# Other slots for the side work of two state-space scans: softplus additions, MLP halves, the parts of B, output additions, and one SiLU

## The chip, the cores and the metric

The kernel is one program on one core of a Trainium2 chip. Its inputs and outputs lie in the chip's memory. The metric is the device time of a whole execution in microseconds (us), the median of several runs; lower is better.

## The reference, cut to what matters

Four images of 256 channels and 64 x 64 points pass through four layers, each with a residual addition. Layers 0 and 1 are attention layers, which the change does not touch. Layers 2 and 3 are state-space ("Mamba") layers; layer 3 treats the 256 channels as four groups of 64 that share their weights, and an MLP follows its scan. What the scan computes in both, for every channel d and each of 16 states n:

```python
delta = softplus(dt @ dt_proj_w + dt_proj_b)      # dt, B, C: projections of u
h     = exp(delta * A[n]) * h + (delta * u) * B[n]   # over the 4096 points
y    += C[n] * h                                     # summed over n
y     = (y + u * D) * silu(z)                        # then out_proj
```

In the grouped layer there follow, per group, a normalisation, `gelu(m @ fc1 + b) @ fc2`, and at the end a 256 x 256 convolution with SiLU and the residual addition.

## The kernel before, in words

The four images are computed one after the other: two attention layers, the first state-space layer (`mamba_layer`), the grouped one (`grouped_mamba_layer`). All data are float32 on 128 partitions (channels); a stretch of 1024 points is a chunk, half of it (512) is what one matmul writes.

**Slots.** `scan_blocks` runs both scans. A block is 128 channels of one chunk; a slot is one state n of one block, so a layer has 16 blocks x 16 slots = 256 slots for an image. In a slot, VectorE multiplies delta*u into B's row (`pb`, L915) and runs the recurrence (`h`, L921); GpSimd multiplies by C (`hc`, L927); TensorE adds `hc`, transposed, into PSUM (`turn`, L873, tile `y`); ScalarE makes the decay of a slot three ahead (`da`, L857) and keeps the last column of the slot before (`m_state`, L862). TensorE spreads B's row over the partitions (`spread`, L845) two slots ahead. In three of a block's 16 slots, those in `apart` (0, 4 and 8 in the grouped layer), the row of B comes by DMA instead (tile `bb`) and GpSimd multiplies it (L831), issued two slots ahead; the decay of these slots goes to PSUM (`dap`).

**Order.** The schedule is manual: every engine's order is the order of the program text. A slot issues, in this order: `pb`, `h`, the GpSimd product for slot i+2, `hc`, the decay for slot i+3, `m_state`, the DMA loads of C and B, the background steps of the slot, `spread` for i+2, `turn` for i-1, and `dap` for i+2. In slot 1 of a block (`ends[0]`) the copies of the previous block's y out of PSUM (L884) stand behind the background steps; y has one buffer, so the new block's first `turn` waits for them.

**Background steps.** `blk["bg"]` is a dictionary from slot to steps; `put(block, slots, steps)` fills it by hand. The steps that matter here:

- `x_proj` (through `table_steps`): projections to B, C and dt (tile `m_bct`), then B split in bf16 parts: ScalarE copies (`m_parts`, L1082) and GpSimd subtractions (L1085), in turn: copy, subtraction, copy, subtraction.
- `delta` (`delta_steps`): for each half of the chunk a matmul (`dt_ps`), three ScalarE functions (L1044 to L1046) and VectorE's addition (L1050), which also ends the use of the PSUM buffer; then delta*u on GpSimd (L1054).
- `mlp`: out projection and its square (L1654, L1655), the deviation (L955, L956), a scale on GpSimd (L1664), first MLP half (`hidden(0)`, `gelu(0)`), second half (`hidden(1)`, `gelu(1)`), then `fc2` in two steps. `hidden` needs both buffers of the PSUM tag `mm`, so the second half's matmuls wait for the first half's GELU.
- `out_conv`, `out_silu`, `out`: the closing convolution, its SiLU, the addition of x on GpSimd (L1743) and the store, which SyncE issues in its own order.
- `silu`: SiLU of z or u, between two loads of ScalarE's function tables.

In the grouped layer two blocks, an "even" and an "odd" one, form a pair (chunk k, column c); an image has 8 pairs, numbered 0 to 7, of 32 slots. The even block's slots carry `x_proj` and `delta` of the odd block, the MLP of the pair before, and for c = 1 the output of the chunk before and the normalisation of the chunk to come; the odd block's slots carry u, `x_proj` and `delta` for the next pair's even block.

Of the kernel before, what the change touches and what calls it, by code (L numbers as in the profile page):

```python
# [8 lines left out]
F32 = mybir.dt.float32  # L9
# [9 lines left out]
P = 128  # L19
# [8 lines left out]
NT = 512  # L28
# [16 lines left out]
class Net:  # L45
# [757 lines left out]
    def scan_blocks(self, blocks, loop, psum, psb, psy, apart, ends, first, last=None):  # L803
# [109 lines left out]
        for i, (blk, n) in enumerate(slots):  # L913
            if not is_apart(i):
                nc.vector.tensor_tensor(pb[i], blk["du"], pb[i], ALU.mult)  # L915
            h[i] = loop.tile([P, NC], F32, tag="h", name="h", bufs=3)
            for ss in pieces(i):
                state = 0.0 if blk["first"] else blk["state"](n)
                if ss.start:
                    state = h[i][:, ss.start - 1 : ss.start]  # L920
                nc.vector.tensor_tensor_scan(  # L921
                    h[i][:, ss], da[i][:, ss], pb[i][:, ss], state, ALU.mult, ALU.add
                )
            product(i + 2)
            hc[i] = loop.tile([P, NC], F32, tag="hc", name="hc", bufs=3)
            for ss in pieces(i):
                nc.gpsimd.tensor_tensor(hc[i][:, ss], h[i][:, ss], cb[i][:, ss], ALU.mult)  # L927
            decay(i + 3)
            keep(i - 1)
            load_c(i + 3)  # L930
            load_b(i + 4)
            if i >= DS and n != ends[0]:
                end(slots[i - DS][0], n)
            for step in blk["bg"].get(n, ()):
                step()
            if i >= DS and n == ends[0]:
                end(slots[i - DS][0], n)
            spread(i + 2)
            turn(i - 1)
            decay(i + 2, True)  # L940
            for d in (pb, da, cb):
                del d[i]
# [173 lines left out]
    def mamba_layer(self, x, bridge, pe_dram, w_in, w_cw, w_x, w_dt, w_out, v_dram):  # L1116
        tc, nc = self.tc, self.nc
        ND = 4
        with ExitStack() as ctx:
# [122 lines left out]
            def silu(*what):  # L1242
                def step():
                    for k, d, key in what:
                        t = chunks[k]["blocks"][d][key]
                        nc.scalar.activation(t, t, AF.Silu)
                    self.exp_ln_tables()

                return step
# [102 lines left out]
            for k in range(n_chunk):  # L1352
# [3 lines left out]
                def put(d, where, steps):  # L1356
                    for i, f in zip(where, steps):
                        bg[d].setdefault(i, []).append(f)
# [5 lines left out]
                        put(0, where, out_proj(k - 1, i // 2, i % 2))  # L1364
                put(0, (9, 10, 11, 12, 12), delta(k, 1))
                put(0, (14, 15), (in_z(k, 0, 0), in_z(k, 0, 1)))
                put(1, (1,), (silu((k, 0, "zs")),))
                put(1, (6, 7, 8, 9, 10), delta(k, 2))
                put(1, (11, 12), (in_z(k, 1, 0), in_z(k, 1, 1)))
                put(1, (14,), (silu((k, 1, "zs")),))  # L1370
# [127 lines left out]
    def grouped_mamba_layer(self, x, bridge, begun, ws_dram, outc_dram, v_dram, out_b, load):  # L1498
        tc, nc = self.tc, self.nc
        w_in, w_cw, w_x, w_dt, w_out, w_f1, w_f2 = ws_dram  # L1500
        with ExitStack() as ctx:
# [140 lines left out]
            def mlp(k, c, s):  # L1642
                ss = slice(s * NT, s * NT + NT)
                box = {}
# [33 lines left out]
                            box["hid"][:, f, g], box["ps"][g], AF.Gelu, bias=f1b[:, f : f + 1]  # L1678
                        )

                def fc1():
                    box["hid"] = work.tile([P, 2, 2, NT], F32, tag="hid", name="hid", bufs=1)
                    gelu(0)
                    hidden(1)
                    gelu(1)
                    self.exp_ln_tables()

                def fc2(f):
                    if f == 0:
# [16 lines left out]
                        )  # L1706

                return (
                    out_proj, deviation, scale, lambda: hidden(0), fc1,
                    lambda: fc2(0), lambda: fc2(1),  # L1710
                )


# [145 lines left out]
            for i, (k, c) in enumerate(pairs):  # L1859
# [12 lines left out]
                if more:  # L1872
# [2 lines left out]
                    put(even, (0, 1, 4, 5, 6), h0)  # L1875
                    put(even, (14, 15), h1)
                    put(odd, (1, 2, 3), h1[2:])
                put(even, (4, 5, 6, 7, 8, 9), x_proj(k, 2 * c + 1))
                if i:
                    m0, m1 = mlp(*pairs[i - 1], 0), mlp(*pairs[i - 1], 1)  # L1880
                    put(even, (5, 6, 7, 10, 11, 12, 13), m0)
                    put(even, (6, 7, 8), m1)
                    if c == 0:
                        put(even, (14, 15), m1[3:])
                        put(odd, (0, 1), m1[5:])
                    elif i + 1 < len(pairs):
                        put(odd, (15,), m1[3:])
                        late.append(((0, 1, 1), m1[4:]))
                    else:
                        put(odd, (3, 4, 5, 6), m1[3:])  # L1890
                put(even, (7, 8, 8, 9, 10), delta(k, 2 * c + 1))
                also = [lambda k=k: out_silu(k - 1)] if c == 1 and k else []
                if i == 0:
                    put(even, (1, 2), [in_z(0, 0, s) for s in range(2)])
# [2 lines left out]
                    also = [lambda blk=odd: silu_of(blk, "u")]  # L1897
                put(even, (3,), (silu(k, c, "zs", also),))
                if c == 1 and k:
                    put(even, (4, 4, 5, 5), [out(k - 1, *sm) for sm in outs])  # L1900
                    put(even, (8,), [lambda k=k: load(slice((k - 1) * NC, k * NC))])
                if c == 0 and k:
                    put(odd, (10, 12, 15), [out_conv(k - 1, *sm) for sm in outs[:3]])
                    late.append(((0,), [out_conv(k - 1, *outs[3])]))

                if i + 1 < len(pairs):
                    nk, ncol = pairs[i + 1]
                    put(odd, (4, 5, 6, 7), all_u(nk, ncol))
                    put(odd, (7,), (silu(nk, ncol, "u"),))
                    put(odd, (8, 8, 8, 9, 10, 11), x_proj(nk, 2 * ncol))  # L1910
                    put(odd, (9, 10, 10, 11, 12), delta(nk, 2 * ncol))
                    put(odd, (13, 14), [in_z(nk, ncol, s) for s in range(2)])
            self.scan_blocks(
                [blk for c in chunks for blk in c["blocks"]], loop, psum, psb, psy, (0, 4, 8),
# [164 lines left out]
```

## Time and profile before

| | |
|---|---|
| median of 3 runs | 12054.86 us (12047.85 to 12070.48) |
| the profiled execution's own time | 12068.31 us |
| its span in the profile | 12066.5 us |
| VectorE (DVE) busy | 9840.1 us, 82% |
| TensorE (PE) busy | 9882.3 us, 82% |
| GpSimd (POOL) busy | 8887.9 us, 74% |
| ScalarE (ACT) busy | 7053.7 us, 58% |
| scan of the first state-space layer, first image | 1028.4 to 1968.5, 940.1 us |
| scan of the grouped layer, first image | 2023.0 to 2991.4, 968.4 us |

Busy times are shares of the whole span; the four images repeat the same pattern. "Idle before <-X" names what ended an engine's idle time. PE's busy time is that of pipelined matmuls and says little about how near its limit it is. In the lines of a timeline the columns are the start (us from the span's start), the duration, the engine, the line of the code, the operation, what it writes and reads, how many were merged, and the idle time before it with its releaser.

### The profile page before, as it was taken

What the parts mean: (1) busy time and instruction counts of PE and PEld (TensorE: products, weight loads), DVE (VectorE), ACT (ScalarE), POOL (GpSimd) and SP (SyncE); (2) the same over time, 40 slices, a digit from 0 to 9 for tenths busy, and PEclk for the clock granted to TensorE, in tenths of its full rate; (3) what the DMA queues carried; (4) which work ended last, traced back from release to release, by engine and by line L of the source; (5) the groups of instructions that cost most, each with busy time, mean ns of one, the idle gap of its engine ahead of it and who ended that gap; (6) DMA issues with size and microseconds to landing.
All of it is one profiled execution on the core that took longest, in us unless ns stands there. A gap on an engine that the chain in (4) does not pass through costs nothing. (4 is left out here: it accounts for less than half of the span.)

```text
span 12066.5 us, 192470 instructions
## 1 busy us (share of the span) xinstructions
PE 9882.3 (82%) x70624; PEld 5634.8 (47%) x71104; DVE 9840.1 (82%) x8322; ACT 7053.7 (58%) x13064; POOL 8887.9 (74%) x6082
## 2 busy tenths in 40 slices
PE   8887887777888888777789878877778987887777
PEld 4554554444455455444445545544434554554443
DVE  6667998988666799898866679989886677998898
ACT  4555554776455555477645555547764565555776
POOL 3666886888366688688836668868883666886887
PEclk9998998999999899899899989989999998998899
DMA  3343554454334455445433445544543344554444
GB/s 92 103 126 136 172 175 145 168 175 159 86 102 125 136 173 174 146 169 177 156 86 105 123 135 173 174 147 168 175 159 86 103 127 135 173 176 145 169 171 152
DMA packets 682832, 1742.12 MB, mean 144 GB/s; under 512 B 89217, under 2 KB 195217, under 8 KB 681633
## 3 DMA queue, kind: packets, MB, share of 16 engines
q1 hardware_dynamic: 676768, 1721.39, 43.9%
q8 instruction: 563, 9.22, 0.3%
q10 hardware_dynamic: 5120, 8.39, 0.3%
q14 instruction: 381, 3.11, 0.1%
HBM read 1601.51 MB, written 94.37 MB: 141 GB/s over the span
## 5 line engine op out<-in xcount | busy, mean ns | idle before, releaser
L927 POOL TENSOR_TENSOR hc<-h,cb 128x1024 f32<-128x1024 f32 x2056 | 4813.0, 2350 | 908.1 <-DVE h L921 383.3
L921 DVE TENSOR_TENSOR_SCAN h<-da,m_state,pb 128x1024 f32<-128x1024 f32 x1248 | 2920.2, 2340 | 161.9 <-DVE pb L915 2.9
L873 PE MATMUL y<-ident,hc 128*128 128x128 f32 x16384 | 2340.8, 291 | 373.2 <-POOL hc L927 246.9
L873 PEld LDWEIGHTS y<-ident,hc 128*128 128x128 f32 x16384 | 2065.1, 151 | 983.2 <-POOL hc L927 402.4
L915 DVE TENSOR_TENSOR pb<-du,pb 128x1024 f32<-128x1024 f32 x1672 | 2024.8, 1211 | 103.2 <-PE pb L845 72.0
L857 ACT ACTIVATE da<-delta,m_v 128x1024 f32<-128x1024 f32 x1672 | 1898.4, 1141 | 163.0 <-DVE h L921 147.1
L845 PE MATMUL pb<-m_parts,pick 128*128 128x512 bf16 x2832 | 965.4, 411 | 817.6 <-DVE h L921 759.3
L519 POOL TENSOR_SCALAR pr<-pr,sm,zero 128x256 f32<-128x256 f32 x2048 | 1126.4, 568 | 429.4 <-DVE sm L516 381.3
L504 ACT ACTIVATE pr<-sc,mn 128x256 f32<-128x256 f32 x2048 | 959.6, 493 | 728.0 <-DVE mn L493 396.2
L845 PEld LDWEIGHTS <-pick 128*128 128x128 bf16 x3312 | 256.6, 100 | 1824.9 <-DVE h L921 1069.9
L921 DVE TENSOR_TENSOR_SCAN h<-da,pb 128x1024 f32<-128x1024 f32 x424 | 969.7, 2287 | 55.8 <-DVE pb L915 1.9
L831 POOL TENSOR_TENSOR bb<-du,bb 128x1024 f32<-128x1024 f32 x376 | 889.3, 2365 | 76.9 <-DMA bb<-m_cd 70.8
L493 DVE TENSOR_REDUCE mn<-sc 128x4 f32<-128x1024 f32 x512 | 609.4, 1219 | 361.8 <-PE sc L483 361.5
L921 DVE TENSOR_TENSOR_SCAN h<-dap,m_state,bb 128x1024 f32<-128x1024 f32 x288 | 671.8, 2333 | 69.8 <-ACT dap L857 59.1
L532 PE MATMUL pt_ps<-ident,pr 128*128 128x128 f32 x4096 | 591.8, 286 | 134.2 <-ACT pts L545 99.3
L204 PE MATMUL conv_ps<-att_y,att_wb 128*128 128x512 f32 x1536 | 692.9, 595 | 5.3 <-DVE gn_mean L151 5.3
L532 PEld LDWEIGHTS pt_ps<-ident,pr 128*128 128x128 f32 x4096 | 461.5, 145 | 361.5 <-POOL tap L225 93.6
L857 ACT ACTIVATE dap<-delta,m_v 128x1024 f32<-128x1024 f32 x376 | 419.7, 1116 | 357.1 <-DVE h L921 283.5
L483 PE MATMUL sc<-kv,q 32*64 32x128 f32 x16384 | 407.4, 300 | 156.6 <-DMA kv<-kv_dram 103.7
L558 PE MATMUL ov_ps<-pts,kv 128*32 128x64 f32 x16384 | 432.6, 233 | 121.5 <-DVE pts L543 72.7
L240 DVE SCALAR_TENSOR_TENSOR lp<-vimg,att_v,lp 128x512 f32<-128x512 f32 x616 | 465.6, 756 | 28.3 <-DVE lp L240 1.0
L204 PE MATMUL conv_ps<-att_xn,att_wa 128*128 128x512 f32 x1024 | 461.0, 603 | 14.2 <-POOL att_xn L180 14.2
(289 smaller groups left out, 17008.8 us busy)
## 6 DMA issues: line engine op xcount, KB each, us to landing
cb<-m_cd SPq DMA_DIRECT2D x2048, 512.0 KB
kv<-kv_dram SPq DMA_DIRECT2D x1984, 128.0 KB
bb<-m_cd SPq DMA_DIRECT2D x376, 512.0 KB
kv_dram<-kst SPq DMA_DIRECT2D x128, 256.0 KB
kv_dram<-vn SPq DMA_DIRECT2D x128, 256.0 KB
q<-q SPq DMA_DIRECT2D x256, 128.0 KB
m_pe<-in_pe_dram SPq DMA_DIRECT2D x32, 512.0 KB
out_dram<-yo SPq DMA_DIRECT2D x64, 256.0 KB
```

The source lines that it names most:

```text
L204: nc.tensor.matmul(ps, w[:, k, w0 + m * P : w0 + (m + 1) * P], src[:, k], start=(k == 0), stop=(k == 1),)
L493: nc.vector.tensor_reduce(mn[h], sc[h].rearrange("p r w m n -> p (w m) r n"), AX.XY, ALU.min)
L504: nc.scalar.activation(t[:, g].rearrange("p j r t -> p r j t"), sc[h][:, :, g // 2, g % 2, :].rearrange("p r (j t) -> p r j t", j=2), AF.E ...
L519: nc.gpsimd.tensor_scalar(t[:, g], t[:, g], s[:, g : g + 1], self.zero, ALU.mult, ALU.add)
L532: nc.tensor.transpose(pt[h][j][:, g, :], t[:, g, j].rearrange("p r t -> p (r t)"), self.ident,)
L831: nc.gpsimd.tensor_tensor(pb[i], slots[i][0]["du"], pb[i], ALU.mult)
L845: nc.tensor.matmul(pb[i][:, ss], self.pick[:, n : n + 1].to_broadcast([P, P]), blk["parts"][:, ss], start=True, stop=True,)
L857: nc.scalar.activation(da[i], blk["delta"], AF.Exp, scale=blk["a"](n))
L873: nc.tensor.matmul(blk["y"][:, ss], t[:, ss], self.ident, is_transpose=True, start=(n == 0 and ss.start % NT == 0), stop=(n == DS - 1 and ...
L915: nc.vector.tensor_tensor(pb[i], blk["du"], pb[i], ALU.mult)
L921: nc.vector.tensor_tensor_scan(h[i][:, ss], da[i][:, ss], pb[i][:, ss], state, ALU.mult, ALU.add)
L927: nc.gpsimd.tensor_tensor(hc[i][:, ss], h[i][:, ss], cb[i][:, ss], ALU.mult)
```

## The change

A background step may now stand at n + 0.5: it is issued between `spread` and `turn` of its slot. The SiLU of z in the first layer moves from slot 1 to 1.5 of a chunk's second block, behind the copies of y. In the grouped layer the step `fc1` is cut in two, of which the second half stands half a slot or a slot later; the parts of B in the even block move from slots 6, 7, 8, 9 to 9, 11, 12, 13; the first softplus addition moves from slot 8 to 9 (even) and 10 to 11 (odd), beside the second; the four output additions, with their stores, go from slots 4, 4, 5, 5 to 4, 5, 6, 7; and one closing convolution goes from slot 10 to 9 of the odd block. The numbers of instructions are the same on every engine; only their order differs.

```diff
@@ scan_blocks
             spread(i + 2)
+            for step in blk["bg"].get(n + 0.5, ()):
+                step()
             turn(i - 1)
@@ mamba_layer
-                put(1, (1,), (silu((k, 0, "zs")),))
+                put(1, (1.5,), (silu((k, 0, "zs")),))
@@ grouped_mamba_layer, mlp
-                def fc1():
-                    box["hid"] = work.tile([P, 2, 2, NT], F32, tag="hid", name="hid", bufs=1)
-                    gelu(0)
-                    hidden(1)
-                    gelu(1)
-                    self.exp_ln_tables()
+                def fc1(f):
+                    if f == 0:
+                        box["hid"] = work.tile([P, 2, 2, NT], F32, tag="hid", name="hid", bufs=1)
+                    else:
+                        hidden(1)
+                    gelu(f)
+                    if f:
+                        self.exp_ln_tables()
...
-                    out_proj, deviation, scale, lambda: hidden(0), fc1,
-                    lambda: fc2(0), lambda: fc2(1),
+                    out_proj, deviation, scale, lambda: hidden(0), lambda: fc1(0),
+                    lambda: fc1(1), lambda: fc2(0), lambda: fc2(1),
@@ grouped_mamba_layer, the slots
-                put(even, (4, 5, 6, 7, 8, 9), x_proj(k, 2 * c + 1))
+                put(even, (4, 5, 9, 11, 12, 13), x_proj(k, 2 * c + 1))
...
-                    put(even, (5, 6, 7, 10, 11, 12, 13), m0)
+                    put(even, (5, 6, 7, 10, 11, 11.5, 12, 13), m0)
                     put(even, (6, 7, 8), m1)
                     if c == 0:
-                        put(even, (14, 15), m1[3:])
-                        put(odd, (0, 1), m1[5:])
+                        put(even, (14, 15, 15.5), m1[3:])
+                        put(odd, (0, 1), m1[6:])
                     elif i + 1 < len(pairs):
                         put(odd, (15,), m1[3:])
-                        late.append(((0, 1, 1), m1[4:]))
+                        late.append(((0, 0.5, 1, 1), m1[4:]))
                     else:
-                        put(odd, (3, 4, 5, 6), m1[3:])
-                put(even, (7, 8, 8, 9, 10), delta(k, 2 * c + 1))
+                        put(odd, (3, 4, 4.5, 5, 6), m1[3:])
+                put(even, (7, 9, 8, 9, 10), delta(k, 2 * c + 1))
...
-                    put(even, (4, 4, 5, 5), [out(k - 1, *sm) for sm in outs])
+                    put(even, (4, 5, 6, 7), [out(k - 1, *sm) for sm in outs])
...
-                    put(odd, (10, 12, 15), [out_conv(k - 1, *sm) for sm in outs[:3]])
+                    put(odd, (9, 12, 15), [out_conv(k - 1, *sm) for sm in outs[:3]])
...
-                    put(odd, (9, 10, 10, 11, 12), delta(nk, 2 * ncol))
+                    put(odd, (9, 11, 10, 11, 12), delta(nk, 2 * ncol))
```

## The prediction

> **What bounds the kernel now.** From the page's busy times (VectorE and TensorE 82%, GpSimd 74%) I went to busy time by stretch, for the two scans of the first image:
>
> ```profile
> core 0: us, PE busy (x) PEld busy (x) DVE busy (x) ACT busy (x) POOL busy (x), PEclk, DMA share, GB/s
> 1028.40:1968.50 940.10, 799.07 (x3462) 464.47 (x3522) 878.30 (x543) 510.41 (x746) 798.44 (x353) 0.94 0.50 173
> 2023.00:2991.40 968.40, 734.92 (x3425) 407.40 (x3485) 873.45 (x531) 663.57 (x959) 853.10 (x387) 0.91 0.51 171
> ```
>
> The grouped scan has no more VectorE work than the first (873 against 878 us), yet takes 28 us longer. VectorE sets the pace (90% busy), but GpSimd is close behind (88%): what VectorE gains can be lost again to GpSimd. So next, who VectorE waits for in the grouped stretch (us, times, longest):
>
> ```profile
> DVE delta L1050 <- ACT delta L1046: 31.6, 19, 2.5
> DVE h L921 <- ACT dap L857: 12.5, 4, 4.2
> DVE pb L915 <- PE pb L845: 11.5, 8, 4.6
> DVE pb L915 <- PE f_ps L1670: 6.6, 4, 2.2
> DVE m_zs L887 <- PE fin_ps L898: 3.3, 5, 1.0
> ```
>
> About 65 us an image, half of it the softplus addition. The same query in the first layer shows 4.0 us of `m_zs` on `fin_ps` for this image. The rest of the reading is from timelines of the second image. ScalarE and VectorE, pair 3 (c = 1), even block, slots 6 to 9:
>
> ```profile
> 5426.54 1.52 ACT L1005 ACTIVATE m_xn<-m_xn,m_v 128x512 f32<-128x512 f32 x2 [0.96 <-POOL m_xn L998]
> 5427.97 1.04 ACT L1082 ACTIVATE m_parts<-m_bct 128x1024 bf16<-128x1024 f32 x1
> ...
> 5431.10 1.12 ACT L857 ACTIVATE dap<-delta,m_v 128x1024 f32<-128x1024 f32 x1
> ...
> 5432.33 2.35 DVE L921 TENSOR_TENSOR_SCAN h<-dap,m_state,bb 128x1024 f32<-128x1024 f32 x1 [4.26 <-ACT dap L857]
> 5436.85 0.69 DVE L1050 SCALAR_TENSOR_TENSOR delta<-dt_ps,delta 128x512 f32<-128x512 f32 x1 [2.17 <-ACT delta L1046]
> ```
>
> ScalarE works almost without a pause and is late; a copy of parts stands in front of `dap`. The odd block of the same pair, slots 10 and 11:
>
> ```profile
> 5503.96 0.63 ACT L1046 ACTIVATE delta<-delta 128x512 f32<-128x512 f32 x1
> 5504.62 0.69 DVE L1050 SCALAR_TENSOR_TENSOR delta<-dt_ps,delta 128x512 f32<-128x512 f32 x1 [2.48 <-ACT delta L1046]
> 5507.84 0.63 ACT L1046 ACTIVATE delta<-delta 128x512 f32<-128x512 f32 x1
> 5508.81 0.67 DVE L1050 SCALAR_TENSOR_TENSOR delta<-dt_ps,delta 128x512 f32<-128x512 f32 x1
> ```
>
> The second logarithm ends at 5508.47, 0.3 us before its addition starts: the second addition has almost no slack.
>
> **What the Trainium skill says.** "PSUM — Partial Sum Buffer", section "Engine vs sequencer instructions": ScalarE, VectorE and GpSimd take instructions strictly first in, first out, and matmuls keep program order. The trace agrees: `dap` at 5431.10 stands behind work that nobody needs yet. "ScalarE: Activation LUTs", "What ACT_TABLE_LOAD costs": about 1283 ns a load; here 1.28 us, and a SiLU with its two loads 3.65 us. "TensorE: Matmul & The Clock Gate", "Part 1: The HAM clock gate": after an idle window of about 3.4 us matmuls run at half rate. The trace agrees: after PE idles 4.33 us at 5579 to 5584, eight transposes take 1.91 us, later 1.04.
>
> **The change part by part.** No instruction is added or removed on any engine, so every part is a wait that goes, stays or comes.
>
> *Even block, c = 1 (pairs 3, 5).* Copy of the first parts from slot 6 to 9: 1.04 us less ahead of `dap`. One addition of x on GpSimd (1.26) less ahead of the normalisation's scale: the 0.96 wait goes. So `dap` ends 1.9 us earlier, and so does the scan that waits 4.26 for it. The second copy (1.06) also leaves the way of the second half's three functions: their end moves from 5440.86 by 1.9 + 1.05 to about 5437.9. VectorE no longer stops for the first addition; it reaches slot 9's end at about 5437.2, does the first addition (0.67), and waits no more than 0.1 for the second. Both are done near 5438.6 instead of 5441.7: 3.0 us won by slot 10. But GpSimd cannot follow. From 5419.7 to 5466.5 it has one idle gap, 0.85 us, and its work there is unchanged: two subtractions (2.15 + 2.12) leave slots 7 and 9 and come back in 11 and 13, ahead of `bb` for the next block. Its last `hc` of the block can come only 0.85 us earlier. Behind it hang `turn`, the normalisation's matmuls (in program order on PE), the square root on ScalarE, y's copies, `fin_ps` and VectorE's `m_zs` in odd slots 3 and 4. I carry on 1.3 us: 0.85, and some 0.45 because `spread` and the square now come early in this chain.
> *Pair 1* has no output additions, so its 1.01 wait stays; `dap` gains 1.04, and the same chain on GpSimd leaves 0.9. *Pair 7* has no normalisation behind it; there `bb` ends 1 us earlier (GpSimd's 1.02 idle gap), its scan was released 2 us after the present one can be: 1.8.
>
> *Even block, c = 0 (pairs 2, 4, 6).* The copy leaves the queue, and all of the first addition's wait (1.33 to 1.75) goes; the second finds its logarithm done. At slot 15 stands the MLP's first half:
>
> ```profile
> 5583.53 2.65 PE L1670 MATMUL f_ps<-m_sq,m_wf 64*128 64x512 f32 x4 [4.33 <-ACT hid L1677]
> 5586.11 0.61 PE L845 MATMUL pb<-m_parts,pick 128*128 128x512 bf16 x1
> ...
> 5587.19 1.23 DVE L915 TENSOR_TENSOR pb<-du,pb 128x1024 f32<-128x1024 f32 x1 [2.18 <-PE f_ps L1670]
> ```
>
> `spread` waits behind the second half's matmuls, VectorE 2.18 us for it and 1.22 for the next. At 15.5 the matmuls stand behind `spread`: the 2.18 goes; `turn` is 2 us later instead, and `spread` of slot 16 comes about when VectorE wants it (I leave 0.3 to 0.7 of wait). Against it GpSimd's `bb` for odd slot 0, now behind a subtraction, ends at the same time as before: 0.4 of wait. Sum 1.4 + 2.2 + 0.6 - 0.4 - 0.6 = 3.2 (pair 6: 3.0). At 11 and 11.5, and where the halves move across blocks, no VectorE wait existed: nothing, hidden by `spread` two slots ahead.
>
> *Pair 0.* The second addition waits 1.2 for its logarithm behind the second copy: 1.1 goes. Its largest wait (4.6 to 5.5 us for `pb`, behind `x_ps` waiting for SiLU of u) is untouched.
>
> *Odd blocks.* Here the copies of parts stay. From 5492.28 (eviction of u) to 5508.47 ScalarE has no idle, so the second logarithm cannot end sooner. VectorE skips the 2.48, arrives 2.5 earlier at slot 11, and waits some 2.2 there: the wait moves from the first to the second addition. Gain 0.3 in pairs 0, 1, 3, 5; in 2, 4, 6 the convolution ahead of `dt_ps` costs 0.2. The move of the convolution also frees the second `dt_ps` matmul from waiting (1.08 in pair 4) for the PSUM buffer of the first, which the later addition would otherwise lengthen.
>
> Grouped layer, one image: 1.1 + 0.9 + 3.2 + 1.3 + 3.2 + 1.3 + 3.0 + 1.8 + 0.6 = 16.4.
>
> *SyncE's queue.* Stores at slots 6 and 7 hold the loads of C behind them until GpSimd's addition is done, at most some 1.6 us; C is loaded three slots (3 x 3.6 us) ahead: nothing. The tile of `yo` has the one buffer that `hid` takes at slot 11: the last store is issued some 7.5 us before, and the kernel's last store landed within 3 us. Nothing; if that cover went, each us late holds ScalarE at the GELU.
>
> *First layer.* ScalarE and VectorE, second chunk, slots 1 to 3:
>
> ```profile
> 4356.32 1.28 ACT L1246 ACT_TABLE_LOAD   x1
> ...
> 4359.99 1.08 ACT L884 ACTIVATE du<-y 128x512 f32<-128x512 f32 x2
> ...
> 4365.32 0.69 DVE L887 TENSOR_TENSOR m_zs<-fin_ps,m_zs 128x512 f32<-128x512 f32 x1 [2.14 <-PE fin_ps L898]
> ```
>
> y's copies can start when `turn` ends (4356.83), 3.1 us earlier; the 2.14 goes. The SiLU ends some 4361.5, before `m_zs` reads it. By chunk (waits on `fin_ps`): 1.4, 2.1, 1.9 and none: 5.3 an image, with VectorE free of other waits behind, so it stays.
>
> **Sum.** (16.4 + 5.3) x 4 = 87 us. Span 12066.5 - 87 = 11979.5; the profiled execution lies 1.8 us above its span and 13.5 above the median, so 12054.86 - 87 = 11968. What a measurement of this kernel can tell is about 0.2%, 24 us.
>
> **Rivals.** *A, as above*: the odd waits move, GpSimd caps the even ones; gain 40 to 135 us, 11920 to 12015. *B, the waits go altogether*: half of the odd waits too (7 x 1.2 x 4 = 34), and c = 1 keeps its 3.0 (8 x 1.7 = 14), gain 87 + 48 = 135, or 181 if the 11.5 us an image of `pb` on `pb` go as well; 11874 to 11920. For it: the chain has slack at other places; against it: ScalarE's unbroken run. *C, the gains are eaten*: later waits (`fin_ps`, `bb`) take all but the first layer's and a few: 12025 to 12055. *D, slower*: GpSimd idles in slots 8 to 10, where its subtractions were, and is 4.2 us later at `bb` and the block's last `hc`. The present slack of `bb` is 0.8 to 3.3 us; by my working GpSimd idles 0 to 2.9 there. With 2.9 or more in all 32 even blocks, some 2 us are lost in each after slack and first gains: +64 - 21 = +43, about 12098. It decides from an idle time of about 1.5 us beyond what VectorE has won. *E, a step does not do what it says*: only the first layer's or only the MLP's cut acts, -20 to -45: in A's or C's edge.
>
> **Chances.** A 0.64, B 0.13, C with E 0.14, D 0.09. Faster by over 24 us: A, B and a part of C, 0.85; same 0.07; slower 0.08. The range takes A, most of B and the upper edge of C up to 12030: 11895 to 12030; A's own is 11920 to 12015.
>
> **What would show it.** Right: no wait of the first addition; waits of about 2 us at the second addition of odd blocks; `dap` waits of about 2 us in pairs 3 and 5; no `pb` wait on `f_ps`; no `m_zs` wait of 2 us in the first layer; GpSimd above 90% in the grouped scan, which lasts about 952 us, the first 932 to 935. Wrong: GpSimd idle at slots 8 to 10 and `h` waiting for `bb` by over 1 us (D); second additions of odd blocks without wait (B); GELU waiting for a store.

## The result, and the profile after

| | before | after |
|---|---|---|
| median | 12054.86 us | 12005.28 us (11987.04 to 12014.62) |
| the profiled execution's own time | 12068.31 us | 11996.08 us |
| its span | 12066.5 us | 11993.8 us |
| scans of the first state-space layer, mean of the four images | 938.7 us | 938.4 us |
| scans of the grouped layer, mean of the four images | 967.9 us | 951.4 us |

The ratio of the times is 0.9954, with a 95% interval of 0.994 to 0.9969: the kernel is 0.46% faster, some 37 to 72 us with 50 between the medians. The two profiled executions lie 72.2 us apart in their times and 72.7 in their spans, because that of before was 13.45 us above its median and that of after 9.2 us below its own (72.23 - 13.45 - 9.20 = 49.58). Of the 72.7 us, 66.1 are in the four scans of the grouped layer, 1.3 in those of the first layer, and 5 elsewhere.

So the grouped layer gained as much as was forecast (16.5 us an image; the forecast was 16.4), and the first layer did not (0.3 an image; the forecast was 5.3). How much such a mean can tell is seen in kernels whose edit leaves a layer alone: the first layer's scan came to 937.2 to 940.0 us in profiles of kernels that don't touch it (`fc1`, `even`, `odd`, `outs`; 938.7 in before), the grouped scan to 965.0 to 967.3 (`silu`, `light`, `light_silu`; 967.9 in before). A difference of under 1.5 us an image in the first layer, or under 3 in the grouped one, is not clear of that by itself.

Busy time by stretch, the two scans of the first image of after (first layer, then grouped):

```profile
core 0: us, PE busy (x) PEld busy (x) DVE busy (x) ACT busy (x) POOL busy (x), PEclk, DMA share, GB/s
1031.30:1967.70 936.40, 806.89 (x3464) 468.49 (x3524) 878.38 (x543) 510.43 (x746) 798.56 (x353) 0.94 0.49 174
2021.10:2968.80 947.70, 727.18 (x3428) 401.39 (x3486) 873.11 (x531) 662.09 (x959) 852.87 (x387) 0.91 0.51 175
```

The work is unchanged on all engines; the grouped stretch is 20.7 us shorter in this image (14.3 to 16.7 in the others), and GpSimd is now busy for 90% of it. What VectorE waits for in the grouped scan of this image (us, times, longest):

```profile
DVE pb L915 <- PE pb L845: 16.6, 11, 5.5
DVE delta L1052 <- ACT delta L1048: 12.2, 11, 2.3
DVE h L921 <- ACT dap L857: 6.7, 3, 2.2
DVE h L921 <- POOL bb L831: 4.3, 7, 2.3
DVE m_zs L887 <- PE fin_ps L898: 4.0, 8, 0.7
DVE pb L915 <- remote: 2.3, 3, 1.9
```

("remote" stands where the profile does not name what ended the wait.) The softplus addition fell from 31.6 to 12.2 us, the decay `dap` from 12.5 to 6.7, and the 6.6 us of `pb` behind `f_ps` are gone. But `pb` behind B's spread row grew from 11.5 to 16.6, and waits for `bb` grew from 1.3 to 4.3. With the small rows the list sums to 68 us before and 48 in after: VectorE's waits make the whole difference of the two scans.

The even block of pair 3 in the second image, slots 7 to 9, from the timelines of ScalarE and VectorE (the same place as before):

```profile
5398.41 1.52 ACT L1007 ACTIVATE m_xn<-m_xn,m_v 128x512 f32<-128x512 f32 x2
...
5402.02 1.12 ACT L857 ACTIVATE dap<-delta,m_v 128x1024 f32<-128x1024 f32 x1
...
5403.24 2.35 DVE L921 TENSOR_TENSOR_SCAN h<-dap,m_state,bb 128x1024 f32<-128x1024 f32 x1 [2.24 <-ACT dap L857]
...
5409.11 0.67 DVE L1052 SCALAR_TENSOR_TENSOR delta<-dt_ps,delta 128x512 f32<-128x512 f32 x1
5410.32 0.69 DVE L1052 SCALAR_TENSOR_TENSOR delta<-dt_ps,delta 128x512 f32<-128x512 f32 x1 [0.54 <-ACT delta L1048]
```

The copy of parts and the 0.96 us wait of the normalisation are gone from the way to `dap`; the scan waits 2.24 us for it instead of 4.26, the first addition not at all. The odd block of that pair:

```profile
5477.50 0.67 DVE L1052 SCALAR_TENSOR_TENSOR delta<-dt_ps,delta 128x512 f32<-128x512 f32 x1
5480.35 0.69 DVE L1052 SCALAR_TENSOR_TENSOR delta<-dt_ps,delta 128x512 f32<-128x512 f32 x1 [2.18 <-ACT delta L1048]
```

As forecast, the wait of 2.48 at the first addition is now one of 2.18 at the second. And the turn from the even to the odd block in pair 4, where `spread` had waited for the MLP's second half (TensorE, then VectorE):

```profile
5552.29 0.59 PE L845 MATMUL pb<-m_parts,pick 128*128 128x512 bf16 x2 [2.36 <-DVE h L921]
5552.91 1.70 PE L1672 MATMUL f_ps<-m_sq,m_wf 64*128 64x512 f32 x4
5554.73 1.09 PE L873 MATMUL y<-ident,hc 128*128 128x128 f32 x8
...
5554.67 1.21 DVE L915 TENSOR_TENSOR pb<-du,pb 128x1024 f32<-128x1024 f32 x1
```

`spread` goes first, and neither `pb` waits. Here the eight transposes that follow take 1.09 us; before they took 1.91. That turns out to matter.

By pair of the grouped layer, the mean over the four images (us; forecast gains with the odd blocks' terms put in):

| pair | 0 | 1 | 2 | 3 | 4 | 5 | 6 | 7 | sum |
|---|---|---|---|---|---|---|---|---|---|
| before | 119.30 | 122.00 | 120.69 | 124.22 | 121.30 | 124.72 | 119.32 | 116.36 | 967.9 |
| after | 119.61 | 122.03 | 117.41 | 122.46 | 117.01 | 122.21 | 117.05 | 113.60 | 951.4 |
| gain | -0.3 | 0.0 | 3.3 | 1.8 | 4.3 | 2.5 | 2.3 | 2.8 | 16.5 |
| forecast | 1.4 | 1.2 | 3.0 | 1.6 | 3.0 | 1.6 | 2.8 | 1.8 | 16.4 |

### The profile page after: what moved, and what is told of

It is laid out like the page before. It is cut to its first block, busy times and chain, and to the rows that moved or that the text cites. A ratio compares the mean times of both kernels' runs of the same rounds, so it can differ in the third digit from the quotient of the medians.

```text
span 11993.8 us, 192457 instructions
## 1 busy us (share of the span) xinstructions
PE 9862.3 (82%) x70632; PEld 5605.7 (47%) x71104; DVE 9842.8 (82%) x8322; ACT 7047.9 (59%) x13064; POOL 8892.2 (74%) x6082
## 5 line engine op out<-in xcount | busy, mean ns | idle before, releaser
L558 PE MATMUL ov_ps<-pts,kv 128*32 128x64 f32 x16384 | 427.8, 231 | 122.1 <-DVE pts L543 74.1
```

## The experiments

"Scan" below is the mean of the four images' scans in the profiled execution (before: first layer 938.7, grouped 967.9; after: 938.4 and 951.4). Ratios are to the kernel before, on the same chip.

### One part at a time

**silu.** The kernel before with the SiLU's move (and the half slots it needs) alone.

```diff
-                put(1, (1,), (silu((k, 0, "zs")),))
+                put(1, (1.5,), (silu((k, 0, "zs")),))
```

> The kernel before with only the SiLU of the first layer at slot 1.5. Theory (TensorE takes it back): the wait of m_zs on fin_ps in slot 4 of the second block of a chunk (1.4, 2.1, 1.9 us an image) is gone, but pb waits for spread (some 0.7 us at slot 14 of that block) and dap waits longer two blocks on; the first layer's scan keeps 937 to 940 us in every image, the total moves by 0 to -8 us. Rival (the gain is real, and something in the grouped layer lost it): the first layer's scan is 5 us shorter in every image, the total -20 us.

Measured: 12060.93 us, ratio 1.0 (0.9991 to 1.0009); first layer 938.0 us an image, 0.7 less than before and within the spread. So the theory held and the rival fell. What VectorE waits for in the first layer's scan of the first image, before and then in this kernel:

```profile
DVE h L921 <- ACT dap L857: 11.5, 7, 2.9
DVE pb L915 <- PE pb L845: 8.2, 7, 2.8
DVE m_zs L887 <- PE fin_ps L898: 4.0, 2, 2.0
```

```profile
DVE h L921 <- ACT dap L857: 13.1, 8, 2.9
DVE pb L915 <- PE pb L845: 11.9, 12, 2.9
```

The row of `m_zs` is gone, all 4.0 us of it. The other two rows grew by 1.6 and 3.7 us, 5.3 in all; the whole lists, with their small rows, sum to 34.9 and 34.5 us. Over the four images it is 33.7 and 32.5. Where: the timeline of after, second chunk of the second image, ten slots behind the place of the former wait (TensorE, then VectorE):

```profile
4366.89 1.88 PE L1235 MATMUL z_ps<-m_xn,m_wz 128*128 128x512 f32 x4
4368.61 1.88 PE L1210 MATMUL u_ps<-m_xn,m_wxi_w 128*128 128x512 f32 x4
4370.33 0.59 PE L845 MATMUL pb<-m_parts,pick 128*128 128x512 bf16 x2
...
4370.96 1.23 DVE L915 TENSOR_TENSOR pb<-du,pb 128x1024 f32<-128x1024 f32 x1 [0.74 <-PE pb L845]
```

TensorE works through the projections of z and u without a pause, `spread` stands behind them, and VectorE, which now comes earlier, waits. In after and in `silu` alike, the wait for `dap` in the second half of the chunk then grows from 1.3 to some 2.2 us in the second chunk and from 2.4 to 2.9 in the third (means of the four images).

**fc1.** The kernel before with the MLP cut alone.

```diff
-                        put(even, (14, 15), m1[3:])
-                        put(odd, (0, 1), m1[5:])
+                        put(even, (14, 15, 15.5), m1[3:])
+                        put(odd, (0, 1), m1[6:])
...
-                        late.append(((0, 1, 1), m1[4:]))
+                        late.append(((0, 0.5, 1, 1), m1[4:]))
```

> The kernel before with only the MLP's first half cut in two. Theory: the wait of pb on f_ps (2.2 us in pairs 2, 4, 6) and most of the next pb wait are gone; nothing else moves; 3 us in each of these pairs, 9 an image, total -36 us. Rival (GpSimd's bb for odd slot 0 or the later turn takes it): the wait becomes one of h on bb or of m_zs on fin_ps, total 0 to -10 us.

Measured: 12068.11 us, ratio 1.0002 (0.9993 to 1.0011); grouped 968.9. The theory fell; the rival's total about held, but not its cause. The wait of 2.18 us on `f_ps` is gone, but the `pb` of odd slot 2 then waits 3.0 us in pairs 2, 4 and 6, for `spread`. In the grouped scan of the first image of this kernel (11.5 us before):

```profile
DVE pb L915 <- PE pb L845: 15.9, 10, 4.4
```

**even.** The even block's parts of B and first softplus addition alone.

```diff
-                put(even, (4, 5, 6, 7, 8, 9), x_proj(k, 2 * c + 1))
+                put(even, (4, 5, 9, 11, 12, 13), x_proj(k, 2 * c + 1))
...
-                put(even, (7, 8, 8, 9, 10), delta(k, 2 * c + 1))
+                put(even, (7, 9, 8, 9, 10), delta(k, 2 * c + 1))
```

> The kernel before with only the even block's parts of B and softplus addition in their new slots. Theory: pairs 2, 4, 6 gain 1.4 us each, pairs 3 and 5 gain 3 us by slot 10 and keep 1.3 of it because GpSimd runs without idle time from slot 4 to the next block; pairs 0, 1, 7 about 1 each; 10 an image, total -40 us. Rival D (GpSimd idles where its subtractions were and is late at bb): the even blocks end no earlier or later, total 0 to +40 us.

Measured: 12041.51 us, ratio 0.9979 (0.9972 to 0.9987); grouped 962.0, a gain of 5.9 where 10 were expected. Pairs 2, 4 and 6 gained 2.3, 2.8 and 1.5, pair 7 1.6; pair 3 gained nothing, pair 5 1.0, and pairs 0 and 1 lost 1.9 and 1.4. In pairs 3 and 5 slot 8 waits 3.3 us for whichever comes last, `dap` or GpSimd's `bb`: 4.24 less only 0.9. Behind it the chain that the prediction follows from GpSimd's last `hc` shows: `m_zs` in odd slot 4 waits 2.0 us for `fin_ps` there, against 0.5 and 0.9 before.

**odd.** The odd block's first softplus addition and the convolution alone.

```diff
-                    put(odd, (10, 12, 15), [out_conv(k - 1, *sm) for sm in outs[:3]])
+                    put(odd, (9, 12, 15), [out_conv(k - 1, *sm) for sm in outs[:3]])
...
-                    put(odd, (9, 10, 10, 11, 12), delta(nk, 2 * ncol))
+                    put(odd, (9, 11, 10, 11, 12), delta(nk, 2 * ncol))
```

> The kernel before with only the odd block's softplus addition at slot 11 and the convolution at slot 9. Theory (ScalarE's run from the SiLU of u to the second logarithm sets the time): the first addition no longer waits, the second waits 1 to 2.3 us in every odd block, the grouped scan is as long as before within 4 us, total 0 +- 12 us. Rival (the waits of 2.4 us are gone): grouped scan 15 us shorter, total -60 us.

Measured: 12049.58 us, ratio 0.9983 (0.9975 to 0.9991); grouped 964.9, a gain of 3.0. The waits moved to the second addition (1.0 to 2.2 us each), as the forecast had it. In pairs 2, 4 and 6 the `pb` ahead of it now waits 1.3 to 1.4 us as well; with these the odd blocks' waits at this place fell by only 1.0 us an image (16.5 to 15.5), so the rest of the 3.0 has its place elsewhere, at waits that also change from profile to profile.

**outs.** The four output additions alone, from slots 4, 4, 5, 5 to 4, 5, 6, 7.

```diff
-                    put(even, (4, 4, 5, 5), [out(k - 1, *sm) for sm in outs])
+                    put(even, (4, 5, 6, 7), [out(k - 1, *sm) for sm in outs])
```

> The kernel before with only the four output additions at slots 4 to 7. Theory (ScalarE's order sets dap, one addition less ahead of the norm's scale saves the wait of 0.96): the dap wait of pairs 3 and 5 falls from 4.2 to about 3.3 us, the bb wait of pair 7 (1.3 us) goes, 2 to 3 us an image, total -8 to -12 us. Rival (GpSimd's order is not what dap waits for): same waits, total 0 +- 4 us. Second rival: the later store holds the GELU of slot 11, total above +10 us.

Measured: 12067.45 us, ratio 1.0 (0.9991 to 1.0008), so no gain in time; grouped 966.3, a gain of 1.6, nearly all of it in pair 7 (1.8). In pairs 3 and 5 slot 8 now waits 3.18 us instead of 4.24, as expected, but for GpSimd's `hc`, and these pairs end no earlier (-0.1 and 0.3): `m_zs` in odd slot 4 waits 1.7 to 1.9 us.

The parts alone gain, in the grouped layer, -1.0, 5.9, 3.0 and 1.6 us an image: 9.5 of the 16.5 that they gain together. These are readings of one profile for each kernel. The times don't settle it: the ratios of the five parts add up to 0.36%, with 0.07 to 0.09% of doubt on each, and the whole is 0.46% (0.31 to 0.60). That the parts act on one another is read from the places, pair by pair, below.

### Two parts together, and TensorE's rate

**even_fc1.** `even` and `fc1` together.

> The kernel before with the even block's moves and the MLP's first half cut in two together. Alone they gave -6.3 us an image and 0. Theory (with the copies gone, ScalarE reaches the GELU of slot 15 earlier, so spread and the second half's matmuls both come in time): the pb waits of odd slots 1 and 2 in pairs 2, 4, 6 (1.5 to 2 us with the even moves alone, 3 us with the cut alone) are gone, grouped scan 5 us shorter than with the even moves alone, total -45 us. Rival (the two only add): grouped scan as with the even moves alone, total -26 us.

Measured: 12040.96 us, ratio 0.9983 (0.9974 to 0.9992); grouped 962.2, as `even` alone. The theory fell, the rival held: still nothing for the MLP cut. In pairs 2, 4 and 6 the second `pb` of the odd block waits 1.8 us. The same turn of blocks in pair 4 as shown of after (TensorE, then VectorE):

```profile
5576.96 0.59 PE L845 MATMUL pb<-m_parts,pick 128*128 128x512 bf16 x2 [3.16 <-DVE h L921]
5577.58 2.09 PE L1672 MATMUL f_ps<-m_sq,m_wf 64*128 64x512 f32 x4
5579.60 1.97 PE L873 MATMUL y<-ident,hc 128*128 128x128 f32 x8
5581.36 1.44 PE L1697 MATMUL f_ps<-m_xn,m_skip 128*128 128x512 f32 x2
...
5584.38 1.23 DVE L915 TENSOR_TENSOR pb<-du,pb 128x1024 f32<-128x1024 f32 x1 [1.36 <-remote]
```

The order of the work is that of after. But TensorE had been idle for 3.16 us instead of 2.36, and the same matmuls then took 2.09, 1.97 and 1.44 us instead of 1.70, 1.09 and 1.02; the next `spread` comes late, and VectorE waits for it.

I read this place in all 12 cases (pairs 2, 4 and 6 of four images) of each kernel, and sorted them by the rate of the eight transposes:

| kernel | at full rate (about 1.09 us) | their waits of `pb` | at half rate (about 1.97 us) | their waits of `pb` |
|---|---|---|---|---|
| fc1 | none | | 12, after 3.6 us idle | 3.04 |
| even_fc1 | none | | 12, after 3.1 to 3.2 us idle | 1.79 |
| after | 8, after 2.3 to 2.5 us idle | 0.00 | 4, after 3.1 to 3.2 us idle | 1.88 |
| even_fc1_warm (below) | 8, after 1.3 to 2.1 us idle | 0.00 | 4, after 2.1 us idle | 1.38 |

("Full" and "half" are TensorE's granted clock, which these traces record as 1.00 or 0.50.) Within one kernel the wait goes with the rate. That alone is a correlation, so:

**even_fc1_warm.** `even_fc1` with four more matmuls ahead of the gap: those of the hidden layer's first half are issued twice (the list of steps has `hidden(0)` once more as `m1[8:]`, and it writes the same values again).

```diff
-                def hidden(f):
-                    box["ps"] = two("f1_ps")
+                def hidden(f, again=False):
+                    if not again:
+                        box["ps"] = two("f1_ps")
...
-                        put(even, (14, 15, 15.5), m1[3:])
+                        put(even, (14,), m1[3:4])
+                        put(even, (15,), m1[8:])
+                        put(even, (15, 15.5), m1[4:6])
```

> The kernel with the even blocks' moves and the MLP cut, with the matmuls of the hidden layer's first half issued a second time at slot 15 of the even blocks of pairs 2, 4 and 6, ahead of the first output product: the same values are written again, and TensorE is only kept busy there. Theory (after an idle stretch of 3.2 us TensorE runs its next matmuls at half rate, and that is what eats the MLP cut): y's eight matmuls at the next frame take about 1.05 us instead of 1.97, B's product at slot 18 of the pair is no longer waited for (1.7 to 1.9 us before), and the grouped scan falls from 962 to 956 to 958 us an image. Rival (it is the order of the work, not the clock): the wait at slot 18 stays above 1.3 us and the scan at 961 to 963.

Measured: 12022.24 us, ratio 0.997 (0.9957 to 0.9982); grouped 958.5, 3.7 less than `even_fc1`, of which pairs 2, 4 and 6 make 2.8. With more work on TensorE the kernel is no slower and probably faster: its interval and that of `even_fc1` (0.9974 to 0.9992) still overlap, so the place has to show it. The same turn of blocks, pair 4 of the third image:

```profile
8551.47 1.13 PE L1673 MATMUL f_ps<-m_sq,m_wf 64*128 64x512 f32 x4
8554.72 0.59 PE L845 MATMUL pb<-m_parts,pick 128*128 128x512 bf16 x2 [2.12 <-DVE h L921]
8555.33 1.70 PE L1673 MATMUL f_ps<-m_sq,m_wf 64*128 64x512 f32 x4
8557.16 1.09 PE L873 MATMUL y<-ident,hc 128*128 128x128 f32 x8
```

The theory holds in 8 of the 12 cases, where the wait is gone; in the other 4 the half rate came even after 2.1 us of idle time, which I had not expected (the last section shows where these gaps lie). And the size was over-estimated: a wait of 1.4 us less makes a pair only some 0.5 us shorter (117.05 against 117.56), since other waits behind it take part of that back. Even the 4 pairs at half rate are 0.6 us shorter than those of `even_fc1` (118.15), where the wait is only 0.4 us longer. So the rate causes the wait, but explains only a part of the 2.8 us.

### Who takes the first layer's gain

**light** and **light_silu.** The kernel before, and the kernel `silu`, with half of the matmuls that make u in the first layer left out (those of its second 128 input channels), so that u there, and all behind it, is not the reference's.

```diff
-                    for j in range(i % 2 * 2, i % 2 * 2 + 2):
+                    for j in range(i % 2 * 2, i % 2 * 2 + 2) if c == 0 else ():
...
-                            start=(c == 0 and j == 0), stop=(c == 1 and j == 3),
+                            start=(c == 0 and j == 0), stop=(j == 3),
```

> The kernel before with half of the matmuls for u left out in the first layer (those of the second 128 channels, so u of chunks 1 to 3 is computed from half of the input). A control for the next run. Both theories: the first layer's scan is 5 to 10 us shorter than before, since TensorE has 19 us less work a chunk in blocks 1 to 3; the wait of m_zs on fin_ps (about 2 us) in slot 4 of the second block stays.

> The same with half of the matmuls for u left out, and the SiLU at slot 1.5. Theory (in the full kernel TensorE takes the gain back in slots 5 to 15): here it cannot, so the first layer's scan is 4 to 6 us shorter than in the control in every image, -16 to -24 us against it, and no pb wait appears at slot 14. Rival (another engine takes it back, ScalarE before dap or GpSimd): no more than 2 us an image shorter than the control.

Measured: `light` 12030.58 us, ratio 0.997 (0.9958 to 0.9981), first layer 930.1; `light_silu` 12015.23 us, ratio 0.9955 (0.9939 to 0.9972), first layer 923.6. With TensorE relieved the SiLU's move gains 6.6 us an image (every image of `light_silu` is shorter than every one of `light`); with TensorE as it is, 0.7. Waits in the first layer's scan of the first image, `light` and then `light_silu`:

```profile
DVE delta L1050 <- ACT delta L1046: 7.0, 5, 2.4
DVE pb L915 <- PE pb L845: 6.3, 6, 1.5
DVE m_zs L887 <- PE fin_ps L898: 5.8, 3, 2.0
```

```profile
DVE delta L1052 <- ACT delta L1048: 7.2, 5, 2.4
DVE pb L915 <- PE pb L845: 5.5, 4, 2.6
```

The row of `m_zs` goes again, and this time no other row grows by more than 0.2 us: the whole lists sum to 26.4 and 20.0 us. The waits for `dap` (11.5 us before) are missing from both lists: with less work on TensorE they go, so they too hang on TensorE.

### What caps pairs 3 and 5

**noadd.** After without GpSimd's output additions in the first three chunks; the output of these chunks lacks the residual.

```diff
-                    eng.tensor_tensor(yo(k, s, m), xs, yo(k, s, m), ALU.add)
+                    if eng is not nc.gpsimd:
+                        eng.tensor_tensor(yo(k, s, m), xs, yo(k, s, m), ALU.add)
```

> After without GpSimd's output additions in the grouped layer's first three chunks (so that the output there lacks the residual; VectorE's in the last chunk stay). It takes some 4 to 5 us of work from GpSimd's queue in the even blocks of pairs 3, 5 and 7. Theory (in these pairs GpSimd's unbroken run of work is what the scan waits for): pairs 3 and 5 become 1.5 to 2.5 us shorter than after's 122.3, the wait of pair 7 for B's turned copy (2.3 us at slot 16) goes, and the pairs without the additions stay within 0.5 us; 5 to 7 us an image. Rival (another engine stands just behind GpSimd there): pairs 3 and 5 move by less than 0.7 us.

Measured: 11990.93 us, ratio 0.9943 (0.9926 to 0.9959); grouped 948.8, 2.6 less than after. Pairs 3 and 5 became 0.7 and 1.2 us shorter, pair 7 2.0: there the wait for `bb` is gone. But four additions of 1.27 us are 5.1 us of GpSimd's work in each of these blocks, and the wait of slot 8 in pairs 3 and 5 stayed at 2.25. Pairs 0 and 1, where nothing was left out, came out 0.8 us longer than in after, so a pair's 0.7 says little. GpSimd caps pair 7, and pairs 3 and 5 at most in part.

**dapfirst.** After with two moves that take work from ScalarE's way to `dap` in pairs 1, 3 and 5.

```diff
-                    put(even, (0, 1, 4, 5, 6), h0)
+                    put(even, (0, 1, 4, 5, 12), h0)
...
-                    put(even, (6, 7, 8), m1)
+                    put(even, (7, 8, 9) if more else (6, 7, 8), m1)
```

> After with two moves in the even blocks of pairs 1, 3 and 5 of the grouped layer: the next chunk's normalization has its last step (two pieces on ScalarE, 1.5 us together) at slot 12 instead of 6, and the second half's MLP has its first three steps at slots 7, 8 and 9 instead of 6, 7 and 8, so that its two squares (1.2 us) and its logarithm and exponential come behind slot 8's decay on ScalarE. Theory (what pairs 1, 3 and 5 wait for at slot 8, 2.24 us each, is ScalarE's unbroken run of work ahead of the decay, not GpSimd's run of products): the three waits fall below 0.5 us, about half comes back at the additions of slots 9 and 10 and behind, and the grouped scan is 2 to 4 us an image shorter than after's 951, some 8 to 16 us in all. Rival (GpSimd's queue caps these pairs, as the prediction's cap of 1.3 us in them had it): the wait only becomes one for a product or for B's copy on GpSimd, and pairs 3 and 5 stay within 0.5 us of 122.3.

Measured: 12010.58 us, ratio 0.9955 (0.9941 to 0.9968), the same as after; grouped 953.3, pairs 3 and 5 122.1 and 123.1. Waits in the grouped scan of the first image:

```profile
DVE delta L1052 <- ACT delta L1048: 22.9, 11, 4.1
...
DVE h L921 <- POOL bb L831: 5.2, 7, 2.3
```

The row of `dap` is gone, so ScalarE's order did cause that wait. It is replaced by 0.8 us for `bb` and by a second addition that waits 3.2 us instead of 0.5 (pairs 3 and 5). The reason for the latter, from TensorE's timeline in pair 3:

```profile
5419.34 1.02 PE L1661 MATMUL m_pv<-m_sq,one_half 128*128 128x512 f32 x2
5422.68 1.12 PE L1044 MATMUL dt_ps<-m_bct,m_wdt 64*128 64x512 f32 x2 [2.31 <-DVE delta L1052]
```

My move of the MLP's deviation brought `m_pv` between the two `dt_ps`. The PSUM tag `mm` has two buffers; the second `dt_ps` now needs the one that VectorE's first addition reads, and so the addition, moved late by the change, holds up the work for the one behind it. Theory and rival both held in part and neither gained.

### What sets the second addition in the odd blocks

**oddparts.** After with the odd block's copies of parts behind the logarithms, as the change did it in the even block.

```diff
-                    put(odd, (8, 8, 8, 9, 10, 11), x_proj(nk, 2 * ncol))
+                    put(odd, (8, 8, 10.5, 11, 12, 13), x_proj(nk, 2 * ncol))
```

> After with one change: in the grouped layer's odd blocks the two copies of C's rows and ScalarE's pieces around them stand at slots 10.5, 11, 12 and 13 instead of 8, 9, 10 and 11. Theory (ScalarE's unbroken run of work in an odd block's second half is what makes the second addition of the softplus late): the waits of the second addition in odd blocks, 1.0 to 2.3 us each and some 11 us an image, fall to below 0.5 us; part of it comes back as a later B for the next block, so the grouped scan is 4 to 8 us an image shorter than after, 16 to 32 us in all. Rival (the addition waits for TensorE's product, or GpSimd's queue takes it all): the waits of the second addition stay at 1 to 2 us or move one to one to the next block's slot 8 or 16, and the grouped scan is within 1.5 us an image of after's.

(The steps that move are B's parts; the expectation names them by the rows of C.)

Measured: 12054.24 us, ratio 0.9991 (0.9982 to 1.0); grouped 964.0, 12.6 us longer than after. Half of the theory held: the waits of the second addition in the odd blocks, 11.1 us an image in after, went almost altogether (0.3 in pair 1). The size had the wrong sign. Waits in the grouped scan of the first image:

```profile
DVE pb L915 <- PE pb L845: 22.7, 15, 4.3
DVE h L921 <- POOL bb L831: 9.2, 14, 2.1
DVE m_xn L983 <- PE ln_pm L980: 8.1, 3, 3.6
...
DVE delta L1052 <- ACT delta L1048: 3.4, 7, 1.4
```

The move took more than ScalarE's copies with it: two subtractions of GpSimd come with them. The timelines of GpSimd and of TensorE at the end of an odd block (pair 2, second image):

```profile
5387.48 2.13 POOL L1087 TENSOR_TENSOR m_parts<-m_bct,m_parts 32x1024 bf16<-32x1024 f32 x1
5389.58 2.34 POOL L831 TENSOR_TENSOR bb<-du,bb 128x1024 f32<-128x1024 f32 x1
...
5394.28 1.09 PE L873 MATMUL y<-ident,hc 128*128 128x128 f32 x8 [2.54 <-POOL hc L927]
5395.21 3.27 PE L1722 MATMUL oc_ps<-xo,m_woc 128*128 128x512 f32 x4
```

`bb` for the next block stands behind a subtraction of 2.13 us; `hc` and the transposes come late; TensorE is idle for 2.54 us and then runs the convolution in 3.27 us (1.88 us in after); the normalisation's mean and VectorE's subtraction of it follow.

## Why the prediction was right, and where it was wrong

The kernel is faster, and 12005 lies in the range of 11895 to 12030 and in case A's own. The gain of 87 us was 14 too much against the two profiled executions (72.7) and 37 too much against the medians; the 23 between are where these two executions lie beside their medians, not a step of the working. Of the steps, one failed by far the most.

- **The first layer's sum (5.3, "so it stays"): wrong, 0.3 to 0.7 an image, some 20 us over the four.** The mechanism up to the wait was right: y's copies, `fin_ps` and `m_zs` come earlier and all the waits go. The failed term is the reason for keeping it, "VectorE free of other waits behind". A list of VectorE's waits shows no wait behind that place because VectorE was late there. TensorE had no reserve: `silu` shows the 4.0 us of the first image return as 5.3 of `pb` and `dap`, and `light_silu` shows 6.6 us kept once TensorE has less to do.
- **The MLP cut (2.2 + 0.6 of 3.2): wrong as a cost; that its pairs come out right is in part luck.** In pairs 2, 4 and 6 after gained 3.3, 4.3 and 2.3 (forecast 3.0, 3.0 and 2.8). But `fc1` alone gives nothing and `even_fc1` no more than `even`. `even` alone gave 2.3, 2.8 and 1.5 there instead of the forecast 1.0 (1.4 - 0.4), and after is only 1.0, 1.5 and 0.7 shorter than `even`, with all the other moves in it. So the even moves were booked too low and the cut too high. (Which wait the last term of that sum, -0.6, stands for, the working does not say.) The wait that the cut was to end is gone only where TensorE runs at full rate behind the gap, 8 of 12 cases in after. The prediction quoted TensorE's half rate at this very place (4.33 us idle, then 1.91 us), and left it out of the sum. `even_fc1_warm` shows that the rate is a cause of the wait, and its pairs 2, 4 and 6 come to 117.7, 117.3 and 116.7, within 0.4 us of after; of the length of a pair the rate makes some 0.5 us.
- **The odd blocks (0.3 or -0.2 each): the mechanism right, the size off.** Waits of 1.0 to 2.3 us stand at the second additions, as forecast. Alone the part gains 3.0 us an image instead of the forecast 0.6, of which 1.0 is at these waits. In after an odd block of pairs 2, 4 and 6 also waits some 1.4 us for the `pb` just ahead of the second addition, as it does with the part alone, and in pairs 2 and 4 another 0.8 to 1.1 for the `pb` before that. With these the odd blocks of pairs 2, 4 and 6 wait 0.6 to 1.1 us more than before, where the forecast left 0.2.
- **The cap of pairs 3 and 5 (1.3, with the odd block 1.6): right in size (1.8 and 2.5), incomplete in cause.** I named GpSimd alone. The chain behind it shows as forecast: in after `m_zs` of odd slot 4 waits 1.3 us for `fin_ps`. `even` alone leaves 3.3 us of wait at slot 8, shared between `dap` and `bb`; `outs` alone leaves 3.2, for GpSimd's `hc`; only both together come to 2.24, and then it is `dap`. `noadd` and `dapfirst` show that three stand close behind one another there: ScalarE's order, GpSimd's run, and the PSUM buffer of `dt_ps`. Relief of one was worth 1.2 us at most, which is hardly clear of the spread.
- **Pair 0 and pair 1 (1.1 and 0.9): wrong, nothing gained.** The waits named went (the second addition's 1.2; `dap` 3.20 to 2.24, the addition 2.23 to 0.87) and others came: in pair 0 0.5 for `bb` and 0.5 more at the odd block's addition, in pair 1 1.9 for `m_zs` on `fin_ps`. There rival D's mechanism acts in part: in pair 1 GpSimd is idle for 2.2 to 3.8 us at slot 10, where its subtractions had been. **Pair 7 (1.8)** gained 2.8, with a wait for `bb` that is now 2.3 us instead of 1.3.
- **Interaction.** The steps were costed as independent terms. Read from the profiles, alone they give 9.5 us an image in the grouped layer, together 16.5. That the sum came so near owes something to luck, to errors that cancel: the table by pair shows misses of -1.7 to +1.3.

Of what the prediction said would show, the grouped scan of about 952 us (951.4), GpSimd at 90% of it, the second additions' waits, `dap` of about 2 us and the missing `f_ps` wait came true; the first layer's 932 to 935 did not (938.4).

The varying count of half-rate turns is not what spreads after's runs (11987 to 12015). At some 0.5 us a turn, twelve turns make 6 us of these 28 by estimate; and the image of after without any half-rate turn took 953.1 us, the one with two 950.8. What does spread them stays open; the kernel before spreads as much (12044 to 12089 in 47 runs).

## What to carry to other kernels

Before a removed wait is booked as a gain, ask of every other engine how much reserve it has just behind that place: VectorE's list of waits shows none where VectorE is itself late, and the answer lies in the other engine's timeline (does it pause there?). Where two or three engines stand within a microsecond or two of each other, as at slot 8 of pairs 3 and 5, don't add up the edits' gains; cost them together by the place, and try the parts both alone and combined. When the parts sum to the right total, compare them with the measured ones place by place before trusting the working. When a step is moved, move every engine's share of it in the working: a copy on ScalarE brought a 2.1 us subtraction on GpSimd in front of what the next block needs.

## What the runs showed of the hardware

TensorE's rate behind a gap is part of the price of a schedule. At the turn of blocks, in the four kernels of the table, all 28 gaps of 3.1 us and more (12 in `fc1`, 12 in `even_fc1`, 4 in after) were followed by eight transposes in some 1.97 us instead of 1.09; of the 20 shorter gaps 16 were not. The Trainium skill ("TensorE: Matmul & The Clock Gate", "Part 1: The HAM clock gate") says that the rate falls after an idle window of about 3.4 us, and that the window runs freely.

The clock that the traces record agrees with the second: in each of the four kernels (512 to 538 stretches at one rate in each) every stretch but the last, which the program's end cuts off, lasts a whole number of steps of 3.413 us, so the rate changes only on a fixed grid, wherever the work lies. With the first the traces agree only in part. In `even_fc1_warm` nine of the gaps are alike, 2.08 to 2.12 us. The five that began no later than 2.44 us into a step were followed by full rate, the four that began 2.53 us in or later by half: the later a gap begins, the more of it lies in the next step. Two of them, pairs 2 and 4 of the fourth image, with the step in which the gap ends and the one behind it (columns as above; the clock is the third number from the end):

```profile
11314.97:11318.38 3.41, 2.16 (x6) 0.72 (x6) 3.18 (x2) 2.76 (x4) 3.41 (x2) 1.00 0.02 7
11318.38:11321.80 3.42, 3.34 (x11) 2.10 (x10) 3.29 (x3) 3.39 (x6) 3.42 (x3) 0.50 0.49 153
11557.32:11560.73 3.41, 2.27 (x6) 0.72 (x6) 3.15 (x2) 2.76 (x4) 3.41 (x2) 1.00 0.03 12
11560.73:11564.14 3.41, 3.28 (x16) 1.58 (x17) 3.28 (x3) 3.36 (x6) 3.41 (x3) 1.00 0.43 156
```

TensorE was busy for 2.16 of the 3.41 us in the one step and 2.27 in the other, and only the first was followed by half rate: by the profile's busy times, no whole idle step is needed. So work just ahead of a gap is no full protection; it helps or not as the gap falls on the grid. What exactly is counted in a step stays open. Busy time alone is not it: in after, the step from 2551.34 us (pair 4, first image) had only 1.81 us of busy TensorE and was followed by full rate.
